# Gates by channel for pairs of graphs, seven block products in every batch, the norm folded into the projection, and an order written by a list scheduler

## The chip, the cores and the metric

One NeuronCore of a Trainium2 chip. The metric is device time in microseconds of one execution of the whole program; lower is better. All arithmetic is float32.

## The reference

There are 64 graphs of 256 nodes with 256 channels, `x[64, 256, 256]`, and an adjacency `adj[64, 256, 256]`. Two layers are computed, each followed by `layernorm(x + layer(x))`.

```python
# layer 0, on batches of 8 graphs laid end to end (2048 nodes)
h      = relu(bn1(conv1x1(x)))                       # 256 -> 256
x_conv = relu(bn2(conv17(h)) + x)                    # 17 taps along the nodes
s      = x @ w_se.T + b_se                           # 3 coordinates a node
A      = exp(-|s_n - s_m|^2) * adj                   # within a graph
x_nmp  = A @ relu(x @ w_msg.T + b_msg)
gi     = concat(x_conv, x_nmp) @ w_ih.T + b_ih       # 512 -> 3*256
gh     = x @ w_hh.T + b_hh                           # 256 -> 3*256
r, z   = sigmoid(gi_r + gh_r), sigmoid(gi_z + gh_z)
n      = tanh(gi_n + r * gh_n)
x      = layernorm(x + (1 - z) * n + z * x)
# layer 1
h      = layernorm(x) * gamma + beta
x      = layernorm(x + relu(adj @ h @ W_rel + b_rel + h @ W_root))
```

(The reference text names sizes of its own in its setup functions; the arrays used are the ones above.)

## The kernel before, in words

**Stages.** The 17-tap convolution works on 8 graphs at a time (8 batches) and is done as products of small transforms: VectorE splits the batch into 47 products' inputs (`split`, `merge`, `butterflies`, most of it recorded on line L104), TensorE multiplies them by transformed filters (`product`, L396), VectorE merges the results, and TensorE turns them to channels (`channels`, L656). The first batch also builds the transformed filters (`filters`, L212 and L240) and stores them to DRAM, from where later batches load them (`load_w`). This start lasts until the first gate product.

**Per graph** come `messages` (L708), `factors` (a transpose, L742), `distances` (L754, with exp on ScalarE), `mask` (VectorE, L759), `passing` (L766), the gates, `update`, `transposes_h` (L939), `project` (L952) and `aggregate` (L964). A graph's nodes lie as two halves of 128 on the partitions, `n = 0, 1`.

**Gates, graphs 0 to 56 and the last graph.** For each half, `gates_rz` multiplies six input blocks (two of x, two of x_conv, two of x_nmp) as stationary operands by 512 columns of weights, and `gates_n` multiplies the same six by 256 columns. That is 12 products of 512 columns and 12 of 256 a graph. VectorE adds the bias rows while it takes the banks (L788, L798), ScalarE takes tanh (L789).

**Gates, graphs 56 to 62.** `block_gates` (L856) splits inputs and weights into 2 by 2 blocks over node halves and channel halves and uses seven block products in the place of eight, with sums of blocks made on VectorE (`block_sums`, L838 to L841, and `weight_blocks`). The results of graph k and graph k+1 lie in different places (`k % 2`).

**Update and norm.** `update` computes on VectorE, in 512-element instructions, `w = 4n + (z' + 3)(x - n)`; then `bn_stats` and `bn_aggr` (L894, L895) give mean and variance, GpSimd raises to the power -0.5 (L918), VectorE writes the normalized `h` (L926), ScalarE writes `x1` (L929). `transposes_h` turns `h`, ScalarE applies gamma and beta (L941), `project` multiplies it by `[W_rel | W_root]`, 512 columns, and `aggregate` adds `adj @ (h W_rel)` into the same bank.

**Order.** The order of every engine's queue is written out by hand. In the loop over graphs `pump()` is called at ten points and takes steps of the next batch's convolution by costs written into the generators (`cost(n)`, `PE_WEIGHT`, `CONV_WEIGHT`). Steps of graph k-1's projection stand among the gates of graph k. The last graph has a code of its own, `last_graph`, that works in halves. Loads are issued from SP, results are stored from ScalarE's queue.

Of the kernel before, what the change touches and what calls it, by code (L numbers as in the profile page):

```python
# [3 lines left out]

# [25 lines left out]
BG = 8  # L30
# [12 lines left out]
V, U, S, S2, SLOTS = 0, 16, 32, 40, 48  # L43
HP_LEN = M * C * BG * (M + 1)
PE_WEIGHT = 0.3
CONV_WEIGHT = 107.7

LEAVES = [(V + k, V + 8 + k, a) for k, a in enumerate(leaf_angles(PI / 2, 8))]
# [4 lines left out]
SR, ROWS = 32, 36  # L53
OB = 7
HG = 3 * P
# [13 lines left out]
def quarter(th):  # L69

    q = th >= PI / 2
    a = th - PI / 2 if q else th
    return math.tan(a), math.cos(a), q


@with_exitstack
def gnn_two_layers(
# [18 lines left out]
    const = ctx.enter_context(tc.tile_pool(name="const", bufs=1))  # L96
    conv_pool = ctx.enter_context(tc.tile_pool(name="conv", bufs=2))
    psum = ctx.enter_context(tc.tile_pool(name="psum", bufs=8, space=bass.MemoryType.PSUM))

    def bank(name):  # L100
        return psum.tile([P, 512], F32, tag="ps", name=name)

    def stt(o, in0, s, in1, op0=ALU.mult, op1=ALU.add):
        nc.vector.scalar_tensor_tensor(o, in0, s, in1, op0=op0, op1=op1)  # L104


    ctx.enter_context(tc.manual_schedule(engines={
        mybir.EngineType.PE, mybir.EngineType.DVE, mybir.EngineType.Activation, mybir.EngineType.Pool,
        mybir.EngineType.SP}))

    def weight(src, k, n, name, eng, pool=const):
        t = pool.tile([P, k // P, n], F32, name=name, bufs=1)
        eng.dma_start(out=t, in_=src.rearrange("(c p) n -> p c n", p=P))
        return t

    def x_by_tiles(b, nodes, tag="xb"):

        t = conv_pool.tile([P, 4, D], F32, tag=tag, name="xb", bufs=2 if tag == "xb" else 1)
        nc.sync.dma_start(
            out=t, in_=x[b * BG:(b + 1) * BG].rearrange("g (t j) d -> (g t) j d", j=M)[:, nodes, :])  # L120
        return t


    chan_sb = const.tile([P, 8, C], F32)
    nc.scalar.dma_start(out=chan_sb, in_=chan)
    w1 = weight(w1T, D, D, "w1", nc.scalar)

    tb = np.einsum("kf,op->kofp", tap_matrix(), np.eye(OB, dtype=np.float32)).reshape(TAPS * OB, NM * OB)
    tb_dram = nc.inline_tensor(np.ascontiguousarray(tb), name="tap_matrix")
    mhalf = const.tile([P, 8], F32)  # L130
    nc.vector.memset(mhalf, -0.5)
    ones = const.tile([P, P], F32)
    nc.vector.memset(ones, 1.0)

    warm = bank("ps_warm")
    for _ in range(8):
        nc.tensor.matmul(warm[:, :P], ones, ones, start=True, stop=True)
    ident = const.tile([P, P], F32)
    make_identity(nc, ident)


    bn_scale, bn_shift = [], []
    bn2_row = const.tile([P, 2, D], F32)

    def batch_norms():
        for i in range(2):
            g_, b_, m_, v_ = (chan_sb[:, 4 * i + j, :] for j in range(4))
            sc = const.tile([P, C], F32, name=f"bnsc{i}")
            sh = const.tile([P, C], F32, name=f"bnsh{i}")
            nc.vector.tensor_scalar(sh, v_, EPS, None, ALU.add)  # L150
            nc.gpsimd.tensor_tensor(sc, sh, mhalf[:, :C], ALU.pow)
            nc.vector.tensor_mul(sc, sc, g_)
            nc.vector.tensor_mul(sh, m_, sc)
            nc.vector.tensor_sub(sh, b_, sh)
            bn_scale.append(sc)
            bn_shift.append(sh)

    def along_rows(pool, which, row):

        ps = bank("ps_row")  # L160
        for i, v in enumerate((bn_scale[which], bn_shift[which])):
            for c in range(C):
                dg = pool.tile([P, P], F32, tag="dg", name="dg", bufs=2)
                nc.vector.tensor_scalar(dg, ident, v[:, c:c + 1], None, ALU.mult)
                q = i * D + c * P
                nc.tensor.matmul(ps[:, q:q + P], ones, dg, start=True, stop=True)
        nc.scalar.copy(row.rearrange("p i d -> p (i d)"), ps)


    w2m = tc.dram_tile([NM, C, P, D], F32, name="w2m")  # L170
    W2, FIRST = {}, {}

    def store_w2(c):
        for f in range(0, NM, 8):
            g = min(f + 8, NM)
            nc.sync.dma_start(out=w2m[f:g, c].rearrange("f p o -> p f o"), in_=W2[0][:, c, f:g, :])

    def filters(pool):
# [7 lines left out]
        WT = {}  # L186

        def fetch(i):
            if i < len(pieces):
                c, o0, o1 = pieces[i]  # L190
                WT[i] = pool.tile([P, TAPS, o1 - o0], F32, tag="wt", name="wt", bufs=2)
                nc.sync.dma_start(out=WT[i], in_=w2T[c, :, :, o0:o1])

        def scaled(i, starts, early=None):

            c, o0, o1 = pieces[groups[i][0]]
            ws = None if early is not None else pool.tile([P, 4, TAPS, OB], F32, tag="ws", name="ws", bufs=3)
            if early is not None:
                at = (2 + early) * 2
                ws = W2[0][:, 1, at:at + 2].rearrange("p f o -> p (f o)")[:, :4 * TAPS * OB].rearrange(  # L200
                    "p (b k o) -> p b k o", b=4, k=TAPS)
            n, o = len(starts), starts[0]
            nc.vector.tensor_mul(
                ws[:, :n], WT[groups[i][0]][:, :, o - o0:o - o0 + n * OB].rearrange("p k (b o) -> p b k o", o=OB),
                bn2_row[:, 0, o:o + n * OB].rearrange("p (b o) -> p b o", o=OB).unsqueeze(2)
# [3 lines left out]
        def turned(ws, n):  # L209
            ps = bank("ps_tT")  # L210
            for b in range(n):
                nc.tensor.transpose(ps[:TAPS * OB, b * P:(b + 1) * P], ws[:, b].rearrange("p k o -> p (k o)"), ident)  # L212
            tT = pool.tile([TAPS * OB, 4, P], F32, tag="tT", name="tT", bufs=2)
            nc.scalar.copy(tT[:, :n].rearrange("k b p -> k (b p)"), ps[:TAPS * OB, :n * P])
# [3 lines left out]
        yield  # L218
        fetch(1)
        TT = {}  # L220
        WS = {i: scaled(i, groups[i][1]) for i in range(2)}
        yield
        for now in ((2,), (), (3,), (4, 5)):
            for i in now:
                WS[i] = scaled(i, groups[i][1], i - 2)
                if i % 3 == 2:
                    fetch(i // 3 + 2)
            yield
        TT[0] = turned(WS[0], 4)
        for i, (piece, starts) in enumerate(groups):  # L230
# [7 lines left out]
            for a, o in enumerate(starts):  # L238
                ps = bank("ps_w")
                nc.tensor.matmul(ps[:, :NM * OB], TT[i][:, a, :], FIRST["taps"], start=True, stop=True)  # L240
                skip = OB - D % OB if o == D - OB else 0
                pv = ps[:, :NM * OB].rearrange("p (f o) -> p f o", o=OB)
                nc.scalar.copy(W2[0][:, c, :, o + skip:o + OB], pv[:, :, skip:])
            yield

    XF = const.tile([P, S * D + HP_LEN], F32)
    X = XF[:, :SLOTS * D].rearrange("p (s e) -> p s e", e=D)
    HP = XF[:, S * D:].rearrange("p (j c g k) -> p j c g k", j=M, c=C, g=BG)  # L250

    xt_dram = tc.dram_tile([B // 2, P, C, 2 * N], F32, name="xt")
    XC, STAGE = {}, {}
# [4 lines left out]
    def cost(n):  # L258

        return 0.15 + 0.265 * n  # L260

    def halves(base, n, size, second):

# [6 lines left out]
    def split(re, im, size, phis, tmp):  # L270

        h, n = size // 2, len(phis)
        t_re, t_im = tmp, tmp + n * h
        cs = []
        for k, phi in enumerate(phis):
            tan, c, turned = quarter(phi / 2)
            cs.append(c)
# [12 lines left out]
        while k < n:  # L290
            m = k
            while m < n and abs(cs[m] - cs[k]) < 1e-12:
                m += 1
            for base, t in ((re, t_re), (im, t_im)):
# [3 lines left out]
                stt(b, tt, -cs[k], a)  # L298
                yield cost((m - k) * h)
                stt(a, tt, cs[k], a)  # L300
# [3 lines left out]
    def merge(re, im, size, phi, scales, tmp, joint):  # L304


# [4 lines left out]
        if all(abs(x0 - x1) < 1e-12 for x0, x1 in zip(*scales)):  # L311
            for v in (slice(0, 2),) if joint else (0, 1):
                nc.vector.tensor_sub(tt[:, v], a[:, v], b[:, v])
                yield cost(size if joint else h)
                nc.vector.tensor_add(a[:, v], a[:, v], b[:, v])
                yield cost(size if joint else h)
        else:

# [24 lines left out]

# [6 lines left out]
    TREES = [(V, V + 8, 8), (U + 8, U + 12, 4), (U + 4, U + 6, 2)]  # L350
# [7 lines left out]

# [994 lines left out]
```

## Time and profile before

| | |
|---|---|
| median of 3 runs (lowest, highest) | 2219.61 us (2219.22, 2220.58) |
| profiled execution, first to last instruction | 2219.2 us |
| what lies around that span, against the median | 0.4 us |
| TensorE busy, matmuls | 2193.1 us (99%), 8336 instructions |
| TensorE busy, weight loads | 1454.6 us (66%) |
| VectorE busy | 1719.1 us (77%) |
| ScalarE busy | 774.3 us (35%) |
| GpSimd busy | 528.8 us (24%) |
| granted TensorE clock, mean | 0.999 |

The profile comes from one execution. A float32 matmul of the program is two MATMUL records (two passes) and a transpose is one. The duration of a MATMUL record overlaps with the next one's, so a price for a product is read from the distance of starts, as the chain of waits gives it, and not from the mean of a record. VectorE's records overlap a little too.

### The profile page before, as it was taken

What the parts mean: (1) busy time and instruction counts of PE and PEld (TensorE: products, weight loads), DVE (VectorE), ACT (ScalarE), POOL (GpSimd) and SP (SyncE); (2) the same over time, 40 slices, a digit from 0 to 9 for tenths busy, and PEclk for the clock granted to TensorE, in tenths of its full rate; (3) what the DMA queues carried; (4) which work ended last, traced back from release to release, by engine and by line L of the source; (5) the groups of instructions that cost most, each with busy time, mean ns of one, the idle gap of its engine ahead of it and who ended that gap; (6) DMA issues with size and microseconds to landing.
All of it is one profiled execution on the core that took longest, in us unless ns stands there. A gap on an engine that the chain in (4) does not pass through costs nothing.

```text
span 2219.2 us, 24605 instructions
## 1 busy us (share of the span) xinstructions
PE 2193.1 (99%) x8336; PEld 1454.6 (66%) x8336; DVE 1719.1 (77%) x3322; ACT 774.3 (35%) x1594; POOL 528.8 (24%) x933
## 2 busy tenths in 40 slices
PE   9999999999999999999999999999999999999998
PEld 6766776667765676656766567666676657766665
DVE  7967889299874998749986598956889388896675
ACT  6433223532244322433224422243223532234333
POOL 0113222132122321223122231222222132222112
PEclk9999999999999999999999999999999999999999
DMA  5931442315323152233422243222432314421110
GB/s 152 321 132 49 143 137 76 105 38 165 111 77 109 56 177 76 76 105 105 145 88 77 84 133 123 77 95 71 143 111 84 110 43 142 138 77 38 43 34 19
DMA packets 212683, 226.70 MB, mean 102 GB/s; under 512 B 22103, under 2 KB 203854, under 8 KB 212558
## 3 DMA queue, kind: packets, MB, share of 16 engines
q1 hardware_dynamic: 190128, 191.27, 27.3%
q10 hardware_dynamic: 22430, 33.86, 4.4%
q8 instruction: 67, 1.10, 0.2%
q14 instruction: 58, 0.48, 0.1%
HBM read 179.22 MB, written 45.88 MB: 101 GB/s over the span
## 4 chain that ended last, share of the span: by engine, by line
PE 73%; DVE 20%; issue 2%; DMA 2%; POOL 1%; ACT 0%; SPq 0%; POOLq 0%; DVEq 0%
PE ps_k L396 12%; PE ps_rz L785 12%; PE ps_out L952 7%; DVE XF L104 7%; PE ps_rz L782 6%; PE ps_n L797 6%; PE ps_c L518 5%; PE ps_msg L708 4%; PE ps_nmp L766 4%; PE ps_n L795 3%; PE ps_out L964 3%; PE ps_w L240 2%; DMA w<-w2m 2%; DVE XF L466 2%; PE ps_dist L754 1%
## 5 line engine op out<-in xcount | busy, mean ns | idle before, releaser
L104 DVE SCALAR_TENSOR_TENSOR XF<-XF 128x512 f32<-128x512 f32 (+2 forms) x800 | 507.4, 664 | 7.4
L396 PE MATMUL ps_k<-w,XF 128*128 128x256 f32 x1316 | 293.5, 380 | 5.9 <-DMA w<-w2m 4.2
L396 PEld LDWEIGHTS ps_k<-w,XF 128*128 128x128 f32 x1316 | 248.3, 190 | 45.7 <-issue 6.5
L726 POOL TENSOR_TENSOR sq<-st 128x6 f32<-128x6 f32 x64 | 14.1, 221 | 1055.0 <-DVE st L718 1005.5
L789 ACT ACTIVATE rz<-rz 128x512 f32<-128x512 f32 x114 | 71.9, 630 | 445.4 <-DVE rz L788 445.4
L952 PE MATMUL ps_out<-wrr,hT 128*128 128x512 f32 x504 | 226.7, 592 | 0.1
L782 PE MATMUL ps_rz<-whh,xT 128*128 128x512 f32 x456 | 214.7, 593 | 0.1
L785 PE MATMUL ps_rz<-wih,nmp 128*128 128x512 f32 x456 | 214.3, 592 | 0.0
L785 PE MATMUL ps_rz<-wih,xc 128*128 128x512 f32 x456 | 214.3, 592 | 0.0
L798 DVE TENSOR_TENSOR gn<-ps_n,brzn 128x512 f32<-128x512 f32 x114 | 78.0, 684 | 171.1 <-PE ps_n L797 171.1
L929 ACT ACTIVATE x<-w,sh,q 128x256 f32<-128x256 f32 x126 | 68.8, 593 | 400.7 <-POOL sh L921 400.7
L785 PEld LDWEIGHTS ps_rz<-wih,xc 128*128 128x128 f32 x456 | 86.6, 190 | 109.1 <-issue 109.1
L785 PEld LDWEIGHTS ps_rz<-wih,nmp 128*128 128x128 f32 x456 | 86.6, 190 | 109.1 <-issue 109.1
L952 PEld LDWEIGHTS ps_out<-wrr,hT 128*128 128x128 f32 x504 | 95.2, 190 | 93.8 <-issue 81.6
L788 DVE TENSOR_TENSOR rz<-ps_rz,brzn 128x512 f32<-128x512 f32 x114 | 77.5, 680 | 75.9 <-PE ps_rz L785 75.9
L708 PE MATMUL ps_msg<-wms,xT 128*128 128x260 f32 x512 | 131.1, 398 | 0.0
L372 DVE TENSOR_TENSOR XF<-XF 128x512 f32<-128x512 f32 (+3 forms) x128 | 126.1, 1010 | 1.7
L766 PE MATMUL ps_nmp<-AT,msg 128*128 128x256 f32 x512 | 121.0, 379 | 0.0
L782 PEld LDWEIGHTS ps_rz<-whh,xT 128*128 128x128 f32 x456 | 82.1, 190 | 58.6 <-issue 55.0
L964 PE MATMUL ps_out<-hr,adj 128*128 128x256 f32 x504 | 119.6, 380 | 0.0
L795 PE MATMUL ps_n<-whh,xT 128*128 128x256 f32 x456 | 117.2, 379 | 0.0
L797 PE MATMUL ps_n<-wih,nmp 128*128 128x256 f32 x456 | 117.0, 379 | 0.0
(208 smaller groups left out, 3745.1 us busy)
## 6 DMA issues: line engine op xcount, KB each, us to landing
w<-w2m SPq DMA_DIRECT2D x105, 768.0 KB, 5.4
xT<-xt SPq DMA_DIRECT2D x64, 256.0 KB, 3.0
xb<-in_x_dram SPq DMA_DIRECT2D x32, 512.0 KB, 4.2
adj<-in_adjT_dram SPq DMA_DIRECT2D x64, 256.0 KB, 2.7
x<-in_x_dram SPq DMA_DIRECT2D x64, 256.0 KB, 3.0
out_dram<-y ACTq DMA_DIRECT2D x63, 256.0 KB, 2.2
xn<-in_x_dram SPq DMA_DIRECT2D x30, 512.0 KB, 4.3
xt<-xTc ACTq DMA_DIRECT2D x30, 512.0 KB, 3.2
```

The lines of the kernel that those rows point to most:

```text
L104: nc.vector.scalar_tensor_tensor(o, in0, s, in1, op0=op0, op1=op1)
L372: (nc.vector.tensor_add if add else nc.vector.tensor_sub)(sl(o, n), sl(a, n), sl(b, n))
L396: nc.tensor.matmul(ps, X[:, slot, c * P:(c + 1) * P], w(m, c), start=first and c == 0, stop=(c == C - 1), skip_group_check=True)
L518: nc.tensor.matmul(pss[o], w1[:, c, o * P:(o + 1) * P], xTc[:, c, :], start=(c == 0), stop=(c == C - 1))
L708: nc.tensor.matmul(ps[:, :D + 4], XT[k][:, c, m * P:(m + 1) * P], wms[:, c, :], start=(c == 0), stop=(c == C - 1 and not idle))
L766: nc.tensor.matmul(ps[:, d * N:(d + 1) * N], MSG[k][:, m, d * P:(d + 1) * P], AT[k][:, m, :], start=(m == 0), stop=(m == C - 1))
L782: nc.tensor.matmul(prz, XT[k][:, c, q], whh[:, c, 0:2 * D], start=(c == 0), stop=False)
L785: nc.tensor.matmul(prz, ins[i], wih[:, i, 0:2 * D], start=False, stop=(j == 3))
L795: nc.tensor.matmul(pn[:, D:], XT[k][:, c, q], whh[:, c, 2 * D:], start=(c == 0), stop=(c == C - 1))
L797: nc.tensor.matmul(pn[:, :D], t, wih[:, i, 2 * D:], start=(i == 0), stop=(i == 3))
L952: nc.tensor.matmul(ps, hT[:, c, n * P:(n + 1) * P], wrr[:, c, :], start=(c == 0), stop=(c == C - 1))
L964: nc.tensor.matmul(po, ADJ[k][:, m, n * P:(n + 1) * P], hr[:, m, :], start=False, stop=(m == C - 1), skip_group_check=True)
```

## The change

The work is recorded first and ordered afterwards. Every call such as `PE.matmul(...)` makes an `Op` with a key (a wished time), an estimated duration, and dependencies worked out from the cells it reads and writes. `scheduled` then gives each engine's queue its order: it goes forward in time and takes, on the engine that is free first, the ready operation with the smallest key. Keys come from `FIRST_GATES`, `PERIOD` and `GATE_TIME`; the convolution of the next batch is spread over the time of a batch by `spread`. TensorE's banks are shared out: at most 4 for gates, 6 for the rest, 3 for the convolution.

Graphs are handled in 32 pairs by `pair(p)`. Gates are computed by channel: the stationary operand is a 128 by 128 block of weights (`WB`), the moving operand is one channel half of one graph, 256 nodes. The 2 by 2 blocks are now over output halves f, input halves c and the two graphs g of the pair, and each of the seven block products has nine matmuls of 256 columns: four in the first half (gates r and the x part of n), five in the second (z and the rest of n). This holds for all pairs. `RG`, `ZN`, `wT`, `x1`, `HY`, `msg` and `AT` exist once; `xT` twice.

The bias is added by ScalarE while it takes a bank or takes tanh. After the gates, `wT` (w with channels on the partitions) is transposed once (L1209); ScalarE copies it to node order with a sum on the way, and takes the sum of squares (L1217). Line L1237 multiplies `wT` itself, not a normalized `h`, by `[W_rel | W_root]`: gamma, the mean and beta are folded into the weights `wrr` and the row `hrow` at the start, and the scale per node is applied when VectorE takes the bank (L1239). The second norm takes its sum from L1254 on VectorE and its squares from L1260 on ScalarE. Results are stored from SP. `last_graph`, `block_gates`, `block_sums` and `pump` are gone.

```diff
+def scheduled(ops):
...
+        ready = [(t, o) for t, o in times if t <= now + 1e-9]
+        calm = [(t, o) for t, o in ready if t + margin <= now]
+        t, op = min(calm or ready, key=lambda v: (v[1].key - v[1].urgent, v[1].seq))
...
-    def gates_rz(k, n):
-            nc.tensor.matmul(prz, XT[k][:, c, q], whh[:, c, 0:2 * D], start=(c == 0), stop=False)
-            nc.tensor.matmul(prz, ins[i], wih[:, i, 0:2 * D], start=False, stop=(j == 3))
-        nc.vector.tensor_add(rz[:, n, :], prz, brzn[:, :2 * D])
-        nc.scalar.activation(rz[:, n, :], rz[:, n, :], AF.Tanh, scale=0.5)
...
+    for o, a, b, add in ((4, 6, 3, True), (5, 4, 0, False), (6, 0, 6, False), (2, 1, 5, False)):
+        (V.tensor_add if add else V.tensor_sub)(sum_of(o), sum_of(a), sum_of(b))
...
+    for c in range(C):
+        V.tensor_scalar(wrr[:, c, :], wrr[:, c, :], gb[:, 0, c:c + 1], 0.5, ALU.mult, ALU.mult)
+    ps = bank("ps_mean")
+            PE.matmul(ps, ones, wrr[:, c, :], start=(c == 0), stop=(c == C - 1))
+        stt(wrr[:, c, :], ps, -1.0 / D, wrr[:, c, :])
...
+        for v, t, when in zip(ins, (tx, tn, tc_), (due - 28, due - 10, due - 20)):
+            V.tensor_sub(t1, b12, b11)
+            V.tensor_sub(t2, b22, t1)
+            V.tensor_sub(t4, b21, t2)
+            V.tensor_sub(t3, b22, b12)
+            right.append((b11, b21, b22, t4, t1, t2, t3))
+        def product(ps, i, second, start, hold):
+            gates = (((0, (0, 2, 1)), (2, (0,))), ((1, (0, 2, 1)), (2, (2, 1))))[second]
+                        PE.matmul(ps[:, h * N:(h + 1) * N], WB[:, i, s, gate, :], right[s][i], ...)
+            def put(f, g, ps):
+                if second:
+                    A.copy(o, ps)
+                else:
+                    A.activation(o, ps, AF.Identity, bias=bhh[:, 2, f:f + 1])
+            def onto(f, g, ps):
+                V.tensor_add(o, o, ps)
+            a = bank("ps_a", "gate")
+            product(a, 0, second, True, T[:, 0])
+            put(0, 0, a)
+            bb = bank("ps_b", "gate")
+            product(bb, 1, second, True, T[:, 0])
+            onto(0, 0, bb)
+            product(a, 5, second, False, T[:, 1])
+            put(0, 1, a)
+            d = bank("ps_d", "gate")
+            product(d, 4, second, True, T[:, 3])
+            product(a, 6, second, False, T[:, 3])
+            put(1, 1, a)
+            onto(1, 1, d)
+            product(d, 2, second, False, T[:, 1])
+            onto(0, 1, d)
+            product(a, 3, second, False, T[:, 2])
+            put(1, 0, a)
+        stt(gh, r, 1.0, gh, op0=ALU.add, op1=ALU.mult)
+        stt(n, gh, 0.5, n)
+            A.activation(n[:, 2 * f:2 * f + 2], n[:, 2 * f:2 * f + 2], AF.Tanh, bias=bih[:, 2, f:f + 1])
+        V.tensor_sub(r, xT.rearrange("p c g n -> p (c g) n"), n)
+        stt(r, z, 3.0, r, op0=ALU.add, op1=ALU.mult)
+        stt(wT, n, 4.0, r)
...
-            stats(mv, n, w[:, n, :])
-            nc.vector.tensor_scalar(H[k][:, n, :], w[:, n, :], mv[:, n, 0:1], q[:, 1, n:n + 1],
-                                    ALU.subtract, ALU.mult)
+                A.activation(x1[:, g, m, :], ps[:, m * D:(m + 1) * D], AF.Copy, accum_out=total[:, j:j + 1])
+                A.activation(junk, x1[:, g, m, :], AF.Square, bias=total[:, j:j + 1], accum_out=squares[:, j:j + 1])
+                        PE.matmul(ps, wT[:, 2 * f + g, m * P:(m + 1) * P], wrr[:, f, :], ...)
+                stt(HY[:, g, m, :], ps, q[:, 1, j:j + 1], hrow)
```

## The prediction

> **What bounds the kernel now.** I read the page first, for shares, then the chain of waits in order of time around one batch's end, at the first gates and at the end, and last the groups with shapes kept apart, for prices. From the page:
>
> ```profile
> PE 2193.1 (99%) x8336; PEld 1454.6 (66%) x8336; DVE 1719.1 (77%) x3322; ACT 774.3 (35%) x1594; POOL 528.8 (24%) x933
> PE 73%; DVE 20%; issue 2%; DMA 2%; POOL 1%; ACT 0%; SPq 0%; POOLq 0%; DVEq 0%
> ```
>
> TensorE is busy nearly throughout and carries most of the chain. Busy time is modelled for it, so the chain has to show that products stand back to back:
>
> ```profile
> 2000.55 1.72 PE ps_rz L782 x4
> 2002.27 3.43 PE ps_rz L785 x8
> 2005.70 0.87 PE ps_xc L656 x8
> 2006.57 1.73 PE ps_nmp L766 x8
> ...
> 2009.39 1.73 PE ps_n L797 x8
> 2011.11 3.43 PE ps_out L952 x8
> ...
> 2029.99 1.72 PE ps_b L856 x6
> ```
>
> Each piece starts where the one before ends. These are my prices: a product of 512 columns 3.43/4 = 0.858 us, one of 256 columns 1.73/4 = 0.432 (two records each), a transpose 0.87/8 = 0.109, one block product of the old kind 1.72. With them and the counts of the instruction order all products of before sum to 2176.8 us, so TensorE stands still for 42.4 us of 2219.2. They split so: the first gate product starts at 143.65, with 128.2 us of products ahead of it (15.5 idle); the last gate product ends at 2199.8 and the end takes 19.4, with 10.9 of products in it; between lie 2037.7 of products in 2056.1, 18.4 idle. A 1% cut of TensorE's work is worth 1% only while the other engines keep such a queue full.
>
> The start and the end are chains through VectorE and others:
>
> ```profile
> 142.67 0.98 PE ps_xc L633 x7
> 143.65 1.72 PE ps_rz L782 x4
> ...
> 2213.49 0.86 POOL qh L1003
> ```
>
> Prices off TensorE:
>
> ```profile
> L104 DVE SCALAR_TENSOR_TENSOR XF<-XF 128x1024 f32<-128x1024 f32 x96 | 116.2, 1214 | 0.9
> L789 ACT ACTIVATE rz<-rz 128x512 f32<-128x512 f32 x114 | 71.9, 630 | 445.4 <-DVE rz L788 445.4
> L929 ACT ACTIVATE x<-w,sh,q 128x256 f32<-128x256 f32 x126 | 68.8, 593 | 400.7 <-POOL sh L921 400.7
> L953 ACT COPY hr<-ps_out 128x256 f32<-128x256 f32 x126 | 46.7, 371 | 146.8 <-PE ps_out L952 146.8
> L918 POOL TENSOR_TENSOR q<-q,mhalf 128x4 f32<-128x4 f32 x63 | 79.2, 1258 | 5.2
> ```
>
> **TensorE's work.** Gates before: 57 graphs of 12 x 0.858 + 12 x 0.432 = 15.48 us, and 7 of 7 x 1.72 + 4 x 0.432 = 13.77: 978.8. After: 32 pairs x 63 products of 256 columns x 0.432 = 870.9. That is -107.9, all on the path. The transposes of the coordinates halve, 64 x 0.109 = -7.0; the folding adds four products of 512 columns (+3.4) and two bias products (+0.9). Projection, aggregation, messages, distances and convolution keep counts and shapes. After: 2176.8 - 110.6 = 2066.
>
> **VectorE and ScalarE.** VectorE loses bias adds of gates (228 x 0.68), statistics (256 x 0.59) and `h` (126 x 0.41), and gains block sums (384 x 0.415), adds of block products (192 x 0.687) and the scaling at L1239 (128 x 0.687). By mean prices its sum goes from 1883 to 1814; before, that 1883 was 1719 of busy time, because neighbours overlap, so I take 1814 x 0.913 = 1656, 76% of the new span. ScalarE goes from 774 to some 1050 (256 takes of gate banks at 0.59, 640 sums and squares and norms at 0.37 to 0.593). Neither becomes the bound on average; TensorE's stretches cover both. If that cover failed everywhere nothing would be gained, which is a rival below.
>
> No row shows an instruction that also gives a sum. It costs as much as a plain one or up to one small read more, L895's 0.18; I take half, 0.09. Between `wT` and the scale there are 8 of them a pair, 0.7 us, under the projection's 6.9 us on TensorE. The Trainium skill says of this ("VectorE: DVE Perf Modes", Two Vector instructions with no wait between them) that an operation which writes out its accumulator is two instructions; no run here shows it, and by that rule the upper bound would be the one to take, and with 16 such instructions in the end the sum would be 1.4 us more.
>
> **The start.** VectorE works without a gap up to 143, so what it does additionally before the last step of the first convolution delays the gates: sums for the first pair (8 x 0.415), one more mask (0.69), the sums of weight blocks (4 x 1152 elements, 1.35 each): 9.4. First gate product at 153.0, with 136.0 us of products ahead of it.
>
> **The new wait.** `RG`, `ZN` and `wT` exist once. In TensorE's new order the turning of `wT` stands in front of the next pair's first product, and behind the last product of the pair. Between them runs a chain: take of the last bank 0.65, gated sum of 1024 elements 1.22, two tanh of 512 elements 1.35 (L789's 0.630 and a little for a bias), then three dependent 1024-element steps on VectorE at 1.22: 7.3 us in all with handovers. Before, this update was queued beside the next graph's gates and cost nothing. What covers it is what the scheduler put in between:
> - after 21 of the 31 pairs that have a successor, messages passed (3.5) and convolution products (5.2): 8.7, covered;
> - after pairs 4, 8, ... 24, while VectorE still folds and splits the next batch and no convolution product is ready, only 1.73 of passing: 5.6 idle x 6 = 34;
> - after pairs 28, 29, 30, no convolution left, 1.73 again, with four more sums of 0.415 in the chain: 6.1 x 3 = 18;
> - after pairs 0 and 27: 2.2 and 1.1.
> Together 55 us. Tanh and the 1024-element steps have direct rows, so I put this at 45 to 62.
>
> **The end.** From the last gate product: 7.2 for the chain, 0.5 for the first transposes, four copies with sums 1.85, GpSimd 0.25, four squares 2.3, GpSimd 1.5 (power included), by then at 13.6; the projection ends at 15.0; aggregation to 18.5; VectorE 1.6; GpSimd 0.25, squares 2.2, GpSimd 1.2, four norms 4 x 0.593; then 2.9 from there to the end, as before's last step (2216.3 to 2219.2). Sum 29.3, against 19.4 with the halves of `last_graph`.
>
> **The sum.** 153.0 + (2066 - 136 - 11.2 = 1918.4) + 29.3 = 2101; the ordinary stalls of before, 18; the new wait, 55: **2174 us** against the profile's 2219.2. The median is 0.4 us above that span, so this holds for it too. That is -2.0%. Stores moved to SP stand before weight loads there, and every load behind one waits until the norm is done; with 5.4 us to landing and three buffers, as before, I give nothing for it, and up to 0.5 us a pair (16 us) if a load is late. The load of `xT` also has to wait for the chain's subtraction and comes just in time for the messages; its price is in the same 16.
>
> A rule that reads the page otherwise stands in the Trainium skill ("Perfetto Trace Analysis", Identifying the Most-Contended Engine): judge TensorE by the busy share of weight loads, not of matmuls. By it the 66% here would mean a third of headroom and the removed products would be worth little, some 2282 us by this sum; the chain's starts speak against it.
>
> **Rivals.**
> 1. The wait appears at covered places too: convolution products of the cover need a bank freed by VectorE and a weight load, and if they are late, the 21 covered ends cost up to 5.6 each, +118: 2292. It decides from 8 of the 21 on (45 us), and then the kernel is slower. For it: VectorE's queue in the stretch after pairs 4, 8, ... holds 68.3 us at mean prices beside 68.0 of products. Against it: with the overlap above those are 62, and before, convolution products waited for loads for only 4.2 us in all.
> 2. VectorE binds only in those seven stretches, without its overlap, some 4 us each: +28, 2202. Still faster.
> 3. The list order keeps queues fuller than the hand order: ordinary stalls gone, chains a microsecond shorter: 2101 + 45 = 2146.
> 4. The saving does not appear, because products of 256 columns with a new weight block each run slower than 0.432. L797 and L766 are such products and show 0.432; I leave 2%.
>
> **How the numbers follow.** My forecast (2155 to 2195) 52%, rival 3 and below 16%, rival 2 18%, rival 1 12%, rival 4 2%. Forecast, 2 and 3 are faster, 0.86 together, of which I take 0.03 off for the upper edge of rival 2; of rivals 1 and 4, 0.14 together, 0.01 falls on the border. So faster by over 0.2% (below 2215.2; about what a measurement of this kernel can tell) 0.83, within it 0.04, slower 0.13. The range from 2135, below rival 3, to 2220, above rival 2 and into the mild part of rival 1, leaves some 5% and 14% outside.
>
> **What would show it.** In the trace after: gate records of L1150 at 4032 passes with 0.216 from start to start; TensorE idle ahead of L1209, put down to VectorE's `wT`, near 55 us, in nine places of 5 to 6 us; the first L1150 near 153; the end about 29 us after the last L1150; VectorE busy near 1650. Wrong would be: idle before L1209 at nearly every pair (rival 1), idle at L718 or before the adds of L1167 in the stretches after pairs 4k (rival 2), or L1150 slower than 0.216 a pass (rival 4).

## The result, and the profile after

The changed kernel takes **2268.28 us** (median of 4 runs, 2267.24 to 2269.20) against 2220.1 for the kernel before in the same comparison: ratio 1.0216, 95% interval 1.0202 to 1.0231. It is 2.2% slower; the prediction was 2174, faster, with a range from 2135 to 2220.

The page of the changed kernel, to be laid beside the two lines of before (busy time, the granted clock in 40 slices, and the chain by engine):

```profile
PE 2123.0 (94%) x9230; PEld 1659.6 (73%) x9230; DVE 1678.9 (74%) x2966; ACT 1010.7 (45%) x2276; POOL 256.5 (11%) x479
...
PEclk9989999989999999999999999999999999999998
...
PE 75%; DVE 10%; ACT 9%; POOL 4%; issue 2%; SPq 0%; DMA 0%; DVEq 0%; ACTq 0%; POOLq 0%
```

VectorE and ScalarE are close to the forecast (1656 and 1050). TensorE is busy for 94% of a longer span, though 110.6 us of products were taken out, and ScalarE and GpSimd, 1% of the chain of before, carry 13% of this one. What TensorE waited for:

```profile
PE ps_wT L1209 <- DVE wT L1198: 72.5, 15, 9.2
PE ps_a L1150 <- ACT RG L1163: 24.9, 12, 5.3
```

(total us, times, longest). The first line was forecast at 55. The second was not forecast at all: TensorE cannot start the next product in bank `ps_a` of the gates before ScalarE has taken, that is copied out, the product that is in it. (With the waits that appear only on the weight loads and the short ones it comes to 40.1, below.)

These waits alone do not make the loss. One of the forecast waits, at the end of pair 4, cut into stretches (from and to, length, then busy us and count of PE, PEld, DVE, ACT and POOL, then the granted clock, the DMA share and GB/s):

```profile
494.00:500.60 6.60, 6.60 (x32) 5.80 (x31) 6.21 (x9) 2.59 (x4) 0.00 (x0) 1.00 0.13 44
500.60:504.57 3.97, 0.38 (x2) 0.00 (x0) 3.76 (x5) 1.86 (x4) 0.00 (x0) 1.00 0.00 0
504.57:506.67 2.10, 0.00 (x1) 0.00 (x1) 2.07 (x3) 0.00 (x0) 0.00 (x0) 0.51 0.66 170
506.67:511.39 4.72, 4.72 (x15) 4.12 (x16) 4.58 (x13) 3.07 (x13) 0.31 (x1) 0.50 0.09 37
511.39:518.00 6.61, 6.61 (x25) 4.58 (x24) 3.22 (x6) 3.69 (x9) 3.08 (x4) 1.00 0.00 0
```

TensorE starts its last pass before the wait at 500.6 (a pass is one MATMUL record). Four us later, still in the wait, the granted clock falls to 0.50, and it stays there for 6.83 us, 4.72 of them with products. Those run at half speed, so that the wait of 6 us costs 2.4 more afterwards. The records of the clock show 20 such stretches in the changed kernel (15 of 6.8 us, 3 of 3.4, 2 of 10.2) and 2 in the kernel before, one of them behind its last product. The page's row of slices hides this: a slice is 57 us, and 6.8 us at half speed leave it at 0.94.

To split the time I worked from the starts of single passes: a pass of 256 columns takes 0.216 us at full clock and one of 512 takes 0.429; what a pass takes beyond that inside a stretch at 0.5 is put to the clock, up to as much again, and the rest is idle. Single waits are given in the text from the start of the last pass to the start of the next, which is 0.2 us more than the idle time. From the first gate product to the first product behind the last gates:

| kernel | first gate product at | low clock | idle | of it ahead of wT | of it at ps_a |
|---|---|---|---|---|---|
| before | 143.5 | 1.7 | 43.5 | | |
| changed | 167.4 | 33.6 | 152.2 | 73.2 | 40.1 |
| e2_early | 166.6 | 16.0 | 110.9 | 41.3 | 38.8 |
| e3_puts | 165.3 | 26.4 | 120.0 | 83.7 | 15.6 |
| e4_early_puts | 164.3 | 12.7 | 80.1 | 46.0 | 12.1 |
| e5_busy | 166.8 | 9.9 | 92.8 | 14.2 | 40.2 |
| e6_stats_on_vector | 167.6 | 36.3 | 140.2 | 92.4 | 12.5 |
| e9_order_only | 153.3 | 0.2 | 52.1 | 14.0 | 12.7 |
| e12_late_convolution | 165.6 | 3.0 | 55.0 | 22.0 | 11.6 |

The idle time of before, 43.5, is more than the 18.4 of the prediction, mainly because gaps under 0.15 us count here. In e5_busy the products that nobody reads count as work.

### The profile page after: what moved, and what is told of

Its sections match the earlier page's. It is cut to its first block, busy times and chain, and to the rows that moved or that the text cites. A ratio compares the mean times of both kernels' runs of the same rounds, so it can differ in the third digit from the quotient of the medians.

```text
span 2267.3 us, 26151 instructions
## 1 busy us (share of the span) xinstructions
PE 2123.0 (94%) x9230; PEld 1659.6 (73%) x9230; DVE 1678.9 (74%) x2966; ACT 1010.7 (45%) x2276; POOL 256.5 (11%) x479
## 4 chain that ended last, share of the span: by engine, by line
PE 75%; DVE 10%; ACT 9%; POOL 4%; issue 2%; SPq 0%; DMA 0%; DVEq 0%; ACTq 0%; POOLq 0%
PE ps_a L1150 20%; PE ps_k L718 12%; PE ps_d L1150 10%; PE ps_hy L1237 7%; PE ps_b L1150 5%; PE ps_nmp L1127 4%; PE ps_c L836 4%; PE ps_agg L1248 3%; PE ps_msg L1080 3%; PE ps_w L572 2%; PE ps_dist L1114 2%; ACT HY L1268 1%; PE ps_wT L1209 1%; POOL q L1262 1%; ACT junk L1260 1%
## 5 line engine op out<-in xcount | busy, mean ns | idle before, releaser
L718 PE MATMUL ps_k<-cs,XF 128*128 128x256 f32 x1316 | 307.2, 380 | 0.6 <-issue 0.6
L718 PEld LDWEIGHTS ps_k<-cs,XF 128*128 128x128 f32 x1316 | 248.2, 190 | 36.6 <-issue 3.7
L1237 PE MATMUL ps_hy<-wrr,wT 128*128 128x512 f32 x512 | 228.5, 594 | 2.7 <-DVE HY L1239 2.7
L1150 PE MATMUL ps_a<-tx,WB 128*128 128x256 f32 x576 | 180.8, 396 | 26.0 <-ACT RG L1163 24.9
L1237 PEld LDWEIGHTS ps_hy<-wrr,wT 128*128 128x128 f32 x512 | 96.9, 191 | 111.3 <-issue 98.3
L1239 DVE SCALAR_TENSOR_TENSOR HY<-ps_hy,q,hrow 128x512 f32<-128x512 f32 x128 | 95.3, 748 | 101.5 <-PE ps_hy L1237 60.8
L1260 ACT ACTIVATE junk<-HY,total 128x256 f32<-128x256 f32 x128 | 65.4, 511 | 203.8 <-POOL total L1256 200.7
L1150 PEld LDWEIGHTS ps_a<-tx,WB 128*128 128x128 f32 x576 | 105.1, 192 | 62.0 <-ACT RG L1163 37.3
L1248 PE MATMUL ps_agg<-HY,adja 128*128 128x256 f32 x512 | 121.7, 381 | 2.2 <-DVE HY L1239 2.2
L1150 PE MATMUL ps_a<-xc,WB 128*128 128x256 f32 x384 | 120.0, 396 | 0.0
L1248 PEld LDWEIGHTS ps_agg<-HY,adja 128*128 128x128 f32 x512 | 95.9, 190 | 32.0 <-issue 10.9
L1150 PE MATMUL ps_a<-nmp,WB 128*128 128x256 f32 x384 | 119.1, 393 | 0.0
L1127 PEld LDWEIGHTS ps_nmp<-AT,msg 128*128 128x128 f32 x512 | 97.8, 193 | 24.7 <-issue 10.2
L1150 PE MATMUL ps_a<-tc,WB 128*128 128x256 f32 x384 | 114.2, 379 | 0.0
L1150 PE MATMUL ps_a<-tn,WB 128*128 128x256 f32 x384 | 114.2, 379 | 0.0
```

The costliest lines, as they stand in the source:

```text
L718: PE.matmul(ps, X[:, slot, c * P:(c + 1) * P], w(m, c), start=first and c == 0, stop=(c == C - 1), skip_group_check=True)
L1127: PE.matmul(ps[:, d * N:(d + 1) * N], msg[:, g, m, d * P:(d + 1) * P], AT[:, g, m, :], start=(m == 0), stop=(m == C - 1), hold=[nmp[:, :, g]])
L1150: PE.matmul(ps[:, h * N:(h + 1) * N], WB[:, i, s, gate, :], right[s][i], start=start and h == 0 and j == 0, stop=j == len(sources) - 1, sk ...
L1237: PE.matmul(ps, wT[:, 2 * f + g, m * P:(m + 1) * P], wrr[:, f, :], start=(f == 0), stop=(f == C - 1), hold=[HY[:, g, m]], need=[q[:, 1, j: ...
L1239: stt(HY[:, g, m, :], ps, q[:, 1, j:j + 1], hrow)
L1248: PE.matmul(ps[:, n_ * D:(n_ + 1) * D], adja[:, g, m, n_ * P:(n_ + 1) * P], HY[:, g, m, :D], start=(m == 0), stop=(m == C - 1))
```

## The experiments

**Is the low clock a cause?** Products that nobody reads are put into the waits; the order stays. The edit as e5_busy has it:

```
+        turned = [s.real for s in op.spaces if op.engine == "PE" and s.name == "ps_wT"]
+        if turned:
+            for _ in range(WARM.get(turns / 2, 0)):
+                nc.tensor.matmul(turned[0][:, :N], ones.made(), WB[...], start=True, stop=True)
+            turns += 1
+WARM = {0: 20, 4: 12, 8: 12, 12: 12, 16: 12, 20: 13, 24: 12, 28: 12, 29: 12, 30: 12, 31: 14}
```

> The order of work is that of the changed kernel; only at the eleven ends of pairs 0, 4, 8, 12, 16, 20, 24, 28, 29, 30 and 31, where TensorE waits 6 to 10 us for wT, 12 to 20 products of ones with a weight block (256 columns, 0.432 us each) are put in front of the turning of wT, into the bank that it is about to use. Nobody reads them. The wait stays, TensorE only is busy during it. Theory 1 (the granted clock): after each of these waits the trace of the changed kernel shows TensorE at 0.5 for 6.83 us (once 10.24), which is 3.4 us of work lost each, 39 us together; kept busy, it stays at full clock and the kernel takes 2229 to 2240 us, with 8 or 9 slow stretches left of 20. Theory 2 (the waits alone cost the time; the low clock falls into stretches that wait anyway): 2268, or up to 5 us more.

In this first form a condition never held and none of the products was issued. Its 2268.54 us (ratio 1.021) are the changed kernel once more.

> The edit that e1_warm was to make: its products were never issued (the trace has no record of them, and its times are those of the changed kernel). Now 12 to 20 products of ones with a weight block (256 columns, 0.432 us each) stand in front of the turning of wT at the ends of pairs 0, 4, 8, 12, 16, 20, 24, 28, 29, 30 and 31, in the bank that it uses next; nobody reads them. The wait for wT stays as long as it is, but TensorE is busy in it. Theory 1 (the clock): the eleven stretches at 0.5 that follow these waits, 39 us of lost work, go; 2229 to 2240. Theory 2 (the low clock falls where TensorE waits anyway): 2268 or up to 5 us more.

2247.37 us, ratio 1.0099 (1.0082 to 1.0116). Against the changed kernel that is 21 us by the medians and 26 by the ratios, which allow for the kernel before being slower in this comparison. The same wait as above, now filled (timeline, TensorE alone: start, us, what, and in brackets the idle time before):

```profile
497.11 5.34 PE L1322 MATMUL ps_wT<-WB,ones 128*128 128x256 f32 x24
502.96 1.09 PE L1209 MATMUL ps_wT<-ident,wT 128*128 128x128 f32 x8 [0.51 <-DVE wT L1198]
503.88 0.60 PE L1150 MATMUL ps_a<-xT,WB 128*128 128x256 f32 x2
```

The turning takes 1.09 us, where it took 1.97 after the idle wait, and the product behind it 0.60 in place of 1.06. So the clock is a cause, and theory 2 falls. But theory 1 had counted 39 us, half of each whole stretch, and a part of each stretch lies inside the wait itself. By the passes' starts the low clock fell by 25.6 us (start and end included), and that is what came back.

**The forecast wait.** One word for the list scheduler: the first products of a pair no longer count as writers of `RG`.

```
-                                  skip_group_check=True, hold=[hold])
+                                  skip_group_check=True, hold=[hold] if second or i not in (0, 1, 4) else [])
```

> The first block products of a pair for reset and hidden gates (0, 1 and 4) no longer have to stand behind the last reading of RG in the list scheduler; it puts two of them (3.5 us) in front of the turning of wT after pairs 4, 8 ... 24 and three (5.2) after pairs 28 to 30. Theory 1 (waits before wT and the clock): these nine waits of 6.1 to 6.6 us fall to 1 to 2.6, too short for the clock to fall: 37 us of idle time and nine times 3.4 us of low clock less, 2268 - 68 = 2200, of which up to 15 may come back as waits for the take of the first bank. Theory 2 (the chain from the last gate product over wT to the next take sets the pace, so that the wait only moves behind the turning): no more than 10 us gained, 2258 or more.

2206.59 us, ratio 0.9932 (0.9917 to 0.9946), some 62 us gained. Theory 1 holds: idle time ahead of wT falls by 32, the low clock by 18. The waits at ps_a stay (38.8), as they should.

```profile
PE ps_wT L1209 <- DVE wT L1198: 39.2, 13, 13.4
```

Not all of the shortened waits were too short for the clock to fall, as the expectation had said they would be: of the six after pairs 4 to 24, now 2.6 to 3.2 us, four were still followed by 3.41 or 6.83 us at 0.5. Pair 0's grew from 9.6 to 13.8 us.

**The wait that was not forecast.** This is the place in the changed kernel, pair 4 being the next (timeline, all engines, rows in between left out):

```profile
461.03 2.29 DVE L782 TENSOR_TENSOR XF<-XF 128x2048 f32<-128x2048 f32 x1
461.19 2.20 POOL L1256 TENSOR_SCALAR total<-total 128x4 f32<-128x4 f32 x1 [20.03 <-DVE HY L1254]
...
464.63 4.49 DVE L782 TENSOR_TENSOR XF<-XF 128x2048 f32<-128x2048 f32 x2
...
465.86 0.61 ACT L1092 ACTIVATE msg<-msg 128x512 f32<-128x512 f32 x1
...
467.05 2.96 POOL L1262 TENSOR_TENSOR q<-q,mhalf 128x4 f32<-128x4 f32 x1
...
470.75 1.59 ACT L1268 ACTIVATE HY<-HY,sh,q 128x256 f32<-128x256 f32 x3 [4.28 <-POOL sh L1263]
...
472.24 0.67 ACT L1163 ACTIVATE RG<-ps_a,bhh 128x512 f32<-128x512 f32 x1
...
472.96 1.22 PE L1150 MATMUL ps_a<-tx,WB 128*128 128x256 f32 x2 [5.02 <-ACT RG L1163]
```

Read it from below. TensorE waits 5.02 us for ScalarE's take at 472.24. The take stands in ScalarE's queue behind the norms of the pair before (L1268); these wait 4.28 us for GpSimd; and GpSimd needs 2.20 us for a multiplication of four columns and 2.96 for a power while VectorE folds (the power took 1.04 at the end of this run, where VectorE rests). The scheduler had reckoned 0.3 and 1.2, and so took the norms to be ready in time.

```
-                dur = 1.2 if ALU.pow in args else 0.3 + 1.5e-3 * n
+                dur = 3.0 if ALU.pow in args else 1.0 + 1.5e-3 * n
```

> One number of the list scheduler is changed: it reckons GpSimd's small operations at 1.0 us instead of 0.3 and the power at 3.0 instead of 1.2, as the trace shows them beside VectorE's long ones. It then puts the four norms at the end of a pair one take of a gate bank later in ScalarE's queue, so that this take no longer waits for GpSimd. Theory 1 (the 40 us that TensorE waits at ps_a for ScalarE come from norms and sums queued ahead of the take): these waits fall to 10 to 20, the three low clocks that follow them go, and the kernel takes 2230 to 2245. Theory 2 (ScalarE's queue is only late because the products are): 2265 to 2270.

2225.49 us, ratio 1.0016 (1.0006 to 1.0025): 43 us from one changed estimate in a scheduler, more than theory 1 had said. The wait shrinks as expected, and at the place above the take now stands in front of the norms (waits, then ScalarE's timeline):

```profile
PE ps_a L1150 <- ACT RG L1163: 4.1, 4, 1.3
...
465.56 0.69 ACT L1163 ACTIVATE RG<-ps_a,bhh 128x512 f32<-128x512 f32 x1 [1.92 <-PE ps_a L1150]
466.14 0.62 ACT L1092 ACTIVATE msg<-msg 128x512 f32<-128x512 f32 x1
468.05 2.08 ACT L1268 ACTIVATE HY<-HY,sh,q 128x256 f32<-128x256 f32 x4 [1.29 <-POOL sh L1263]
```

By the table 24.5 us of the gain are at ps_a, 7 are low clock and some 18 are short waits elsewhere, while the waits ahead of wT grew by 10.5: the estimate moves more of the order than this one place.

> Both edits: first products ahead of the turning of wT, and GpSimd reckoned slower in the list scheduler. If both waits and the clock that falls after them are the cause, the gains add: 2165 to 2185, below the kernel before, with the granted clock above 0.99 between pairs 1 and 30. If one queue only takes over from the other, 2200 or more.

2172.74 us, ratio 0.9778 (0.9764 to 0.9793). The two gains would add to 104 us and together give 96, and the kernel is now faster than the one before. The granted clock between pairs 1 and 30 is above 0.99, as expected.

**Are ScalarE's sums themselves to blame?** Statistics go back to VectorE.

```
-                A.activation(x1[:, g, m, :], ps[:, m * D:(m + 1) * D], AF.Copy, accum_out=total[:, j:j + 1])
-                A.activation(junk, x1[:, g, m, :], AF.Square, bias=total[:, j:j + 1], accum_out=squares[:, j:j + 1])
+                A.activation(x1[:, g, m, :], ps[:, m * D:(m + 1) * D], AF.Copy)
+                stats(mv, j, x1[:, g, m, :])
```

> Undoes one part in the changed kernel: mean and variance of both norms come from VectorE's statistics of each row again, as before the change, and not from ScalarE's sums. ScalarE loses 256 squares (0.51 us) and 384 reads of an accumulator (0.19 to 0.21), VectorE gains 256 statistics at 0.59 (151 us) and loses 128 reads at 0.08. Theory 1 (GpSimd's steps and the norms behind them hold up the takes, whoever makes the sums; VectorE has no room in the stretches with folds): the waits at ps_a stay, VectorE rises to some 1820 and the kernel takes 2280 to 2320. Theory 2 (ScalarE's sums themselves hold up the takes): 2225 to 2240.

2260.47 us, ratio 1.0159 (1.0144 to 1.0174): neither theory's number. VectorE rose to 1816.5 us as reckoned, and the waits at ps_a went to 12.5, against theory 1. But the wait ahead of wT rose to 92.4, with new waits of 3.5 to 4.3 us at four pairs that were covered in the changed kernel and 6.2 in place of 1.8 at pair 27 (profile: `PE ps_wT L1214 <- DVE wT L1203: 91.5, 18, 9.4`), and the low clock stayed at 36.3. That VectorE is later with the update because of the statistics fits this and is not shown by itself, since the order moved too. In this order the sums' place trades waits at ps_a for waits ahead of wT, and is worth 0.6%.

**The start, and where a batch's convolution stands.** Three edits on top of e4_early_puts, each alone:

```
e7:  -(V.tensor_add if add else V.tensor_sub)(sum_of(o), sum_of(a), sum_of(b))
     +(G.tensor_add if add else G.tensor_sub)(sum_of(o), sum_of(a), sum_of(b))
e11: sums:            prog.at(FIRST_GATES - 6, 0.01)   ->  prog.at(166.4, 0.01)
     gamma and beta:  prog.at(FIRST_GATES + 16, 0.001) ->  prog.at(164.8, 0.001)
e12: -CONV1_FROM, CONV1_TO, CONV_FROM, CONV_OUT, CONV_TO = -32.0, -6.0, -6.0, -36.0, -8.0
     +CONV1_FROM, CONV1_TO, CONV_FROM, CONV_OUT, CONV_TO = -32.0, -6.0, 44.0, -36.0, -8.0
```

> From e4_early_puts, with the four sums of weight blocks (4 x 1152 elements) on GpSimd in place of VectorE. In the changed kernel they take 5.28 us of VectorE ahead of the last step of the first convolution. Theory 1 (VectorE sets the start): the first gate product comes 5 us earlier, at 159, pair 0's wait of 15 us shrinks by as much, and 2172.7 becomes 2158 to 2168. Theory 2 (GpSimd needs so long for them, or slows VectorE so much, that products 2, 4, 5 and 6 wait): 2172 to 2185.

2171.76 us, ratio 0.976 (0.9745 to 0.9774): 1 us less by the medians, 4 by the ratios. Pair 0's wait shrank from 15.4 to 9.7 us, as theory 1 had it, but the first gate product came 6.5 us later, at 170.8. The timeline says why:

```profile
149.19 8.67 POOL L1034 TENSOR_TENSOR WB<-WB 128x1152 f32<-128x1152 f32 x3
149.48 2.84 DVE L1139 TENSOR_TENSOR tn<-nmp 128x256 f32<-128x256 f32 x1
152.24 3.13 DVE L885 SCALAR_TENSOR_TENSOR XF<-XF 128x512 f32<-128x512 f32 x1
155.29 2.84 DVE L1140 TENSOR_TENSOR tn<-nmp,tn 128x256 f32<-128x256 f32 x1
158.17 0.42 DVE L1141 TENSOR_TENSOR tn<-nmp,tn 128x256 f32<-128x256 f32 x1
```

Beside three sums on GpSimd of 2.9 us each, three VectorE steps of 0.42 to 0.69 us take 2.84 to 3.13: each ends just after a sum ends. The Trainium skill states it ("SBUF — State Buffer", Who interferes with whom): the two engines share a read port, and a VectorE instruction with two inputs from SBUF and a GpSimd instruction that reads SBUF exclude each other for a whole instruction. This trace agrees.

> From e4_early_puts, with only two due times moved: the sums of weight blocks (VectorE, 5.28 us) and the folding of gamma and beta are due after the first gates, not before. Theory (VectorE's sums, and the products that follow them, set the start; the rest of the start stays late): first gate product 5 us earlier, at 159; 2172.7 becomes 2158 to 2168, the gain that e7_sums_on_gpsimd missed because its sums on GpSimd held VectorE up. If the start is set by something else, the time stays within 3 us.

2157.86 us, ratio 0.9723 (0.9707 to 0.9739), first gate product at 160.4. Left on VectorE and moved behind the first gates, the sums, with the folding of gamma and beta, give the 15 us that GpSimd could not: the first gate product comes 3.9 us earlier than in e4_early_puts, pair 0's wait falls from 15.4 to 9.7, and between the gates 6.4 us less are lost to the low clock. Which of the two moves gives how much was not tried.

> From e4_early_puts, with one due time moved: the work of the coming batch's convolution after its first layer is due from 44 us after a batch's first gates on, instead of 6 us before them, so that the folds (4 x 2.29 us of VectorE) and the splits no longer stand before the update of pairs 0, 4, 8 ... 24. Theory: the waits before wT of these seven pairs (15.4 us and six of 2.6 to 3.7, with the low clock behind five of them) all fall under 2 us, and 2172.7 becomes 2138 to 2150. Rival (the convolution then ends too late, and its products or the next batch's first gates wait): 2165 or more.

2142.27 us, ratio 0.9646 (0.9632 to 0.9661): 30 us from one due time. The wait of pair 0 falls from 15.4 to 3.9 us, and those of pairs 4 to 24 are at most 1.0. Pair 0 in e4_early_puts and in this run:

```profile
232.49 1.94 PE L1209 MATMUL ps_wT<-ident,wT 128*128 128x128 f32 x8 [14.99 <-DVE wT L1198]
...
224.61 1.94 PE L1209 MATMUL ps_wT<-ident,wT 128*128 128x128 f32 x8 [3.51 <-DVE wT L1198]
```

**All of it.**

```
+FIRST_GATES, PERIOD, GATE_TIME = 136.87, 60.94, 15.8
+CONV1_FROM, CONV1_TO, CONV_FROM, CONV_OUT, CONV_TO = -43.06, 2.08, 44.23, -58.11, -24.04
+PAIR_LEAD, FILTER_LEAD, LOAD_AHEAD = 20.23, 8.43, 1.23
+URGENT = 45.83
+READY = {"PE": 0.14}
...
+        parts = (slice(0, 4, 2), slice(1, 4, 2)) if p == B // 2 - 1 else (slice(0, 4),)
+        for part in parts:
+            r, gh, z, n = RG[:, part, 0, :], RG[:, part, 1, :], ZN[:, part, 0, :], ZN[:, part, 1, :]
```

> e7_sums_on_gpsimd, and: the last pair's update, norms and stores are split by graph; the list scheduler reckons 0.19 us for a read of ScalarE's accumulator; and its due times are moved, above all the convolution of the coming batch, which starts 50 us later after the first gates of a batch and is spread over the rest of it, so that VectorE's folds no longer stand in front of wT of pairs 0, 4, 8 ... 24. If waits before wT, the clock that falls in them, the start and the end are all that is lost: no wait over 3 us before wT but at the end, granted clock 0.99 or more from pair 1 on, 2125 to 2150. If VectorE or ScalarE now binds in the later part of a batch, 2160 or more.

2134.88 us, ratio 0.9594 (0.958 to 0.9608). Ahead of wT only pair 0 and the end still wait for more than 1.1 us. (Beside these lines e8_best has the edits of e2, e3 and e7 and the 0.19 us for a read of the accumulator.) The next run takes GpSimd's sums and the split out again and moves the due times once more.

```
-FIRST_GATES, PERIOD, GATE_TIME = 143.0, 62.0, 18.0
-CONV1_FROM, CONV1_TO, CONV_FROM, CONV_OUT, CONV_TO = -32.0, -6.0, -6.0, -36.0, -8.0
-PAIR_LEAD, FILTER_LEAD, LOAD_AHEAD = 20.0, 15.0, 12.0
+WSUM_AT, HROW_AT = 160.3, 158.68
+FIRST_GATES, PERIOD, GATE_TIME = 136.87, 61.12, 15.97
+CONV1_FROM, CONV1_TO, CONV_FROM, CONV_OUT, CONV_TO = -43.06, 2.08, 71.05, -68.52, -28.59
+PAIR_LEAD, FILTER_LEAD, LOAD_AHEAD = 25.96, 7.29, 1.23
...
+                dur += 0.19 * ("accum_out" in named)
...
-READY = {"PE": 0.7}
+READY = {"PE": 0.1}
```

(The edit of e9_order_only beside those of e2 and e3; e11's two due times stand here as `WSUM_AT` and `HROW_AT`, and `URGENT` goes from 12 to 51.18.)

> The changed kernel with exactly its instructions and tiles, in another order: e4_early_puts, the moved due times of e8_best, and the sums of weight blocks and the folding of gamma and beta into the projection due only after the first gates. The end is not split, and the sums stay on VectorE, since in e7_sums_on_gpsimd VectorE's steps of 0.69 us took 2.98 to 3.12 beside GpSimd's sums of 2.95. Theory (the whole loss of the changed kernel is order: waits before wT, takes behind norms, the start, and the clock that falls in the gaps): first gate product near 158 to 162, 2125 to 2145. Rival (VectorE's and ScalarE's added work itself costs, and e8_best's gain came from its split end and GpSimd): 2150 or more.

**2123.67 us**, ratio 0.9551 (0.9538 to 0.9564), first gate product at 153.3, both a little better than the theory had it; the rival is out. (The 2.98 to 3.12 us that the expectation gives for e7_sums_on_gpsimd stand in e8_best's trace.) Apart from semaphore waits, the counts of every operation on every engine are those of the changed kernel; only the order differs. It is 6.4% faster than the changed kernel and 4.5% faster than the one before:

```profile
PE 2079.9 (98%) x9230; PEld 1635.4 (77%) x9230; DVE 1683.4 (79%) x2966; ACT 1002.5 (47%) x2276; POOL 255.5 (12%) x479
...
PEclk9999999999999999999999999999999999999998
...
PE 89%; DVE 7%; ACT 3%; issue 1%; DMA 0%; POOL 0%; DVEq 0%; ACTq 0%; SPq 0%; POOLq 0%
...
PE ps_wT L1211 <- DVE wT L1200: 11.0, 7, 7.3
```

VectorE and ScalarE work as much as in the changed kernel, TensorE's share of the chain goes from 75% to 89%, and GpSimd is gone from it. Of the 11.0 us ahead of wT, 7.3 are the end.

The same with the `parts` of e8_best:

> e9_order_only with the last pair's update, norms and stores split by graph. In e8_best the end took 32.4 us with the split, as in the changed kernel without it, because the projection there ran at a clock of 0.5. If the split is worth nothing, it equals e9_order_only within 2 us; if the chain of the end is shortened as its sum of steps says, 4 to 6 us less.

2122.25 us, ratio 0.9542 (0.9529 to 0.9555): the split is worth nothing that can be told. It turns the gap of 7.6 us before the last turning into two, of 3.2 and 4.3, and the clock falls all the same: the first half of the last projection takes 5.98 us, the second 3.60.

## Why the prediction was wrong

The sum was 153.0 + 1991.4 (products 1918.4, ordinary stalls 18, new wait 55) + 29.3. The trace has 167.4 + 2067.9 + 32.0: misses of 14.4, 76.5 and 2.7. (Two slips in the working are too small to matter: 20 ends of pairs are covered, not 21, and the terms of the end add up to 29.0.)

**Right.** The prices: 4032 passes of L1150 at 0.216 us from start to start. The loads of VectorE and ScalarE, within 4%. (The list of what VectorE gains and loses adds up to 21 us more, not 69 less; it leaves out the update in longer instructions and the adds of the old block gates, which the total has.) The mechanism of the new wait and its places: nine waits of 6.1 to 6.6 us after pairs 4, 8 ... 24 and 28 to 30, that is 5.9 to 6.4 idle, forecast at 5.6 to 6.1; pair 27 at 1.6, forecast at 1.1. Rival 1 is out, since the covered ends are idle for 0.6 us at most; rival 4 is out by the price.

**The step that failed first: the new wait, "Together 55 us".** Each wait was given its own length and nothing behind it. Between first and last gate 33.6 us of low clock are missing from the sum, and some 9 in the start and the end. Nothing was wrong with the rows used; what they hardly show is the clock, because in the kernel before TensorE never stood still for more than 2.0 us ahead of its last product. Its trace held one sign, a wait of 1.3 us and just after it 3.41 us at 0.5, which the page's row does not show (timeline, then stretches as above):

```profile
1983.69 0.70 PE L754 MATMUL ps_dist<-lr 4*128 4x256 f32 x4 [1.29 <-ACT lr L745]
...
1985.01:1988.42 3.41, 3.41 (x13) 2.71 (x12) 2.96 (x8) 1.22 (x3) 0.54 (x2) 0.50 0.52 156
```

The Trainium skill has the rule ("TensorE: Matmul & The Clock Gate", HAM oscillation): leave no idle gaps of TensorE above some 3.4 us. It speaks directly against a change that makes eleven of 6 to 10 us, and it was the one to weigh; the runs agree with it. They are stricter still: in e4_early_puts four gaps of 2.6 to 3.7 us were followed by 3.41 us at 0.5, while two of 2.8 and 3.2 were not.

**"Neither becomes the bound on average; TensorE's stretches cover both."** On average it is so (45% busy), and still 40.1 us of idle time at ps_a come from its queue. The prediction listed what ScalarE does more of, but not what the take of a first bank stands behind, and it took GpSimd's steps (1.5 us, power included) only at the end, where VectorE rests. e3_puts shows it is the order and not ScalarE's load: same instructions, 43 us.

**Pair 0, forecast 2.2, took 9.6, 9.4 of it idle.** Between the first and the second of the update's last three steps VectorE works 16 us for the next batch: four folds (8.9 us) and six steps of 1024 elements (timeline):

```profile
216.05 1.23 DVE L1196 TENSOR_TENSOR RG<-xT,ZN 128x1024 f32<-128x1024 f32 x1 [1.98 <-ACT ZN L1195]
217.19 8.89 DVE L782 TENSOR_TENSOR XF<-XF 128x2048 f32<-128x2048 f32 x4
226.00 1.22 DVE L609 SCALAR_TENSOR_TENSOR XF<-XF 128x1024 f32<-128x1024 f32 x1
...
233.19 1.22 DVE L1197 SCALAR_TENSOR_TENSOR RG<-ZN,RG 128x1024 f32<-128x1024 f32 x1
234.44 1.23 DVE L1198 SCALAR_TENSOR_TENSOR wT<-ZN,RG 128x1024 f32<-128x1024 f32 x1
...
235.81 1.94 PE L1209 MATMUL ps_wT<-ident,wT 128*128 128x128 f32 x8 [9.22 <-DVE wT L1198]
```

Rival 2 said VectorE's queue binds in the stretches with folds, and put it at some 4 us each. In the changed kernel it binds at pair 0; in e4_early_puts, where the forecast wait is shortened, the same work is also what is left of the waits of pairs 4 to 24, 2.6 to 3.7 us each, and e12_late_convolution takes it away. With 65.9 us (73.2 less 7.3 of the last pair, which the end holds) in place of 55, the wait's term was mis-sized by 11, 7 of them here. The three misses between the gates, 33.6, 40.1 and 10.9, make 84.6; smaller waits and products came out 8 lower than reckoned. The loads behind stores, priced at 0 to 16, show once: 4.0 us for xT at pair 0, where TensorE then had to wait for wT in any case.

**The start, forecast 153.0.** The 9.4 us of added VectorE work were right, and the rest was not seen: the clock falls in a gap of 5.6 us at 129.5 and twice more before the first gates (7.9 us of products lost to it), and hrow's product (2.88 us, 1.88 at full clock in e9_order_only) stands before the first gates. How the 14.4 us divide among these was not tried. That e9_order_only starts its gates at 153.3 shows that the term was within reach of another order.

**The accumulator's read**, taken at half a small read, 0.09: mostly 0.19 to 0.22 us on ScalarE and 0.08 on VectorE, as instructions of their own. So the cited rule, that such an operation is two instructions, holds in this trace; the upper bound that was drawn from it fits ScalarE, the half fits VectorE.

**All of the 94 us missed goes away by order alone.** The waits at ps_a, the low clock and most of the start go away in runs that change no instruction, and the saving of 108 us in gates was there all the time. That e4_early_puts, with the two first repairs, lands on 2173, next to the forecast of 2174, is luck: its start is 11 us later than forecast and 12.7 us are lost to the low clock, while the waits ahead of wT, without the end's, take 39 us and not 55.

## What to carry to other kernels

Price a wait on TensorE at its length plus what the clock loses after it, here 2.4 us for each gap of some 6, and look for gaps of 2.5 us and more first. Average load does not show where a queue is late: for every bank that TensorE reuses, list what stands ahead of its release, on which engine, and what that in turn waits for. Where a list scheduler sets the order, its durations are part of the kernel: take them from the trace, at the place where the neighbours are busy, before judging a change by its time.

## What the runs showed of the hardware

- In the changed kernel the granted clock fell to 0.50 from 2.3 to 5.4 us after a gap of TensorE began, sometimes when products ran again, and returned after 3.41, 6.83 or 10.24 us, mostly 6.83 (after 13.65 or 17.07 behind the longest waits of e2_early, e3_puts and e4_early_puts). Of gaps up to 3.3 us some were followed by it, in the kernel before one of 1.3, and some were not; between the first and the last gate every longer one was. In e5_busy products with unread results kept it at 1.00 through the gap that is shown.
- In the changed kernel GpSimd's operations on four columns took 0.2 us (the power 1.0) with VectorE at rest and up to 2.2 (the power 3.1) beside folds of 2.29; sums of 1152 elements on GpSimd, 2.9 each, stretched VectorE's steps of 0.42 to 0.69 to 2.84 to 3.13.
- A sum that ScalarE gives out with an activation costs a separate read, mostly of 0.19 to 0.22 us; on VectorE it costs 0.08.
